# Source scores of eight end groups looked up two batches early, their rows gathered last, and end batches of 12, 13, 9 and 12 groups

## The chip, the core and the metric

The kernel runs on one core of one Trainium2 chip. The metric is device time in microseconds (us). The engines are named as in the profile: PE is the matrix engine (PEld its weight loads), DVE the vector engine, ACT the scalar engine, POOL the engine that issues the indirect gathers, SP the engine that issues most plain transfers.

## The reference

One graph attention layer over 12,500 nodes and 400,000 edges with 64 features, the edges sorted by destination, and a residual with a layer norm behind it:

```python
h_src = nfeats[src]
h_dst = nfeats[dst]
z_att = jnp.concatenate([h_src, h_dst, efeats], axis=-1)
e = jax.nn.leaky_relu(z_att @ W_attn + b_attn, negative_slope=0.01)[:, 0]
m = jnp.concatenate([h_src, efeats], axis=-1) @ W_ne
emax = jax.ops.segment_max(e, dst, num_segments=N)
ex = jnp.exp(e - emax[dst])
denom = jax.ops.segment_sum(ex, dst, num_segments=N)
alpha = ex / denom[dst]
z = jax.ops.segment_sum(alpha[:, None] * m, dst, num_segments=N)
out = jax.nn.relu(jnp.concatenate([nfeats, z], axis=-1) @ W_out)
return out
...
x = _layernorm(x + _L0_gnn_ref(x, edge_attr_64, ...), axis=-1)
```

## The kernel before, in words

**Groups, lots, batches.** The edges are cut into 782 groups of 512 (128 partitions by 4; the last has 32 partitions). The first 128 groups ("dense") have few destinations and are done without gathering a row per edge. The other 654 groups are worked in 42 batches of up to 16 groups; a batch is four lots of up to four groups. `ENDS` gives the lots of the last batches: (3,3,3,3), (3,3,3,3), (2,2,1,1), and all earlier ones are (4,4,4,4). Batches are numbered from 0, so the last four are 38 (16 groups), 39 (12), 40 (12) and 41 (6). "39.2" below is the lot with index 2 of batch 39.

**One batch.** (a) Gathers: for each group four indirect DMAs on POOL (`gather`, L331) each fetch 128 rows of `table`, which hold a node's source score, its features and two ones, into a `zx` tile. There are eight `zx` tiles, one per lot, so a gather of batch k starts when the same lot of batch k-2 has been multiplied. Up to batch 38 some gathers also wait by hand for marked PE steps of the batch before (`BEHIND`). (b) Scores, lot by lot (`scores`, L371 to L392): ACT copies the destination scores' window and the edge rows, DVE forms edge score + source score (column 0 of `zx`, L381) + destination score. (c) The softmax over the batch, written as a generator that yields four times: it starts with a transpose on DVE (L695) and ends with the transpose at L757. Between them PE turns columns to rows and back (L599, L602), and at each yield `dense_step` puts in other work: up to three pieces of the products of the batch before. (d) Weights (L792) for all lots, then the products on PE: of the first two lots at once, of the other two inside the next batch's softmax (`later`). A group takes four matmuls, in the trace eight passes (L809; in the last two batches L813, in two halves of 64 rows, eight matmuls and sixteen passes), and a lot one small L804 for its ones. (e) `add_in` (L818 to L828) moves the sums of a lot from PSUM to the ring `acc` of node sums, and blocks of nodes that are complete go through `finish0` to `finish3` (PE L1010, L1043, L1053; ACT L1018; DVE L1072 and on).

**The source score by a look.** For the dense groups a source score is not gathered. With src = 128 h + l, ACT makes an indicator over l from a row of the l's (`low_of`, which SP loads broadcast to all partitions; L431, L432), PE multiplies it with the 128 by 98 table of scores (`look_products`, L442: four matmuls, eight passes), and DVE picks the column h and adds it (`look_scores`, L469 to L475). The dense groups' looks end long before the last batches.

**Order.** The order on PE, DVE, ACT, SP and POOL is the order in which the program is written. Each engine takes its instructions in that order, so an instruction that waits holds all behind it.

Of the kernel before, what the change touches and what calls it, by code (L numbers as in the profile page):

```python
# [10 lines left out]
I32 = mybir.dt.int32  # L11
# [5 lines left out]
T = 4  # L17
# [33 lines left out]
NOW = 2  # L51
HALF = 2
# [7 lines left out]
def sorted_path(ctx, tc, x, dst, idx, edge, w_ne, w_attn, b_attn, w_out, out, flag):  # L60
# [29 lines left out]
    ENDS = ((3, 3, 3, 3), (3, 3, 3, 3), (2, 2, 1, 1))  # L90
# [16 lines left out]
    NK = len(sizes)  # L107
    SOON = (starts[1] - 1) // P + 1
# [13 lines left out]
    def kept_at(g):  # L122
        d = round_of(g)
        return g - begins[d] + d % 2 * BD
# [36 lines left out]
    low_rows = dram.tile([DG, P, T], BF16, name="low_rows")  # L161
# [182 lines left out]
    def ahead_of(g0, n, b0):  # L344

        Sk = widths[starts.index(b0)]
        if g0 not in early and b0 == starts[-1]:
            m = follows[g0][1]
            joint_ = edges(g0, n + m)
            early[g0], early[g0 + n] = joint_[:, 0:n], joint_[:, n:n + m]  # L350
# [9 lines left out]
    def rows_of(g0, n):  # L360

        assert g0 + n < NG or n == 1
        return RP if g0 + n == NG else P

    def scores(g0, n, zx, drel, b0, plain):
# [15 lines left out]
        nc.vector.tensor_tensor(ysum[0:r, 0:n], ysum[0:r, 0:n], zx[0:r, 0:n, :, 0], op=OP.add)  # L381
# [83 lines left out]
    def look_scores(g, found):  # L465
# [4 lines left out]
                                high[:, :, g:g + 1].to_broadcast([P, T, NB]), op=OP.is_equal)  # L470
# [330 lines left out]
    def products(k, pg, zx, w, groups, r=P, n=None):  # L801

        if n:
            nc.tensor.matmul(pg[0:1, 0:n, 0:2 * T], ident[0:1, 0:1], zx[0:1, 0:n, :, EW - 1:EW + 1],  # L804
                             start=True, stop=True)
# [60 lines left out]
    nc.sync.dma_start(out=ids, in_=idx[0:DG])  # L866
    nc.sync.dma_start(out=meet, in_=dst[DG * GE - 1:DG * GE + 1].unsqueeze(0))
# [9 lines left out]
    with before:  # L877
# [23 lines left out]
        with tc.manual_schedule(engines={EngineType.DVE, EngineType.Pool, EngineType.Activation, EngineType.PE, EngineType.SP}):  # L901
# [63 lines left out]
            nc.sync.dma_start(out=low_rows, in_=low_row)  # L965
            of_dense = dense_list()
            dense_places(of_dense, fit)
            nc.vector.tensor_copy(of_next[:, 2:4], meet)
# [144 lines left out]
    with loop:  # L1113
# [3 lines left out]
        for k, parts in enumerate(ENDS, len(sizes) - len(ENDS)):  # L1117
            lots[k] = [(starts[k] + sum(parts[:i]), n) for i, n in enumerate(parts)]
        flat = [(g0, n, b0) for b0, lot in zip(starts, lots) for g0, n in lot]
# [15 lines left out]
        def some_products():  # L1135

            if later:
# [3 lines left out]
                products(k, pg, zx, w, range(g, upto), n=n if g == 0 else None)  # L1141
# [27 lines left out]
        with tc.manual_schedule(engines={EngineType.PE, EngineType.DVE, EngineType.Activation, EngineType.SP, EngineType.Pool}):  # L1169
# [14 lines left out]
            for k, G in enumerate(sizes):  # L1184
# [7 lines left out]
                if k:  # L1192
                    joined = resting
                    batch_looks = alike(looks, ())
                    batch_counts = alike(counting)
                    if batch_looks and batch_looks[-1] + 1 in begins:
# [11 lines left out]
                tiles = [ahead.pop(0) if ahead else gather(g0, n, srcs, b0, k == 0, behind_of) for g0, n in lots[k][:3]]  # L1208
                parts = []
                after = node_z = None  # L1210
                for i, (g0, n) in enumerate(lots[k]):
                    if i == 3:
# [639 lines left out]
```

## Time and the profile before

| | |
|---|---|
| median of 3 runs | 4620.77 us (4603.75 to 4627.97) |
| the profiled execution | 4592.69 us |
| its span | 4591.0 us |
| mean granted PE clock | 0.653 of full |
| end of batch 40's softmax to start of batch 41's | 17.82 us |
| start of the last softmax to the end of the span | 41.6 us |

A row of a timeline gives the start in us from the span's start, the duration, the engine, the line and operation, out<-in with shapes, how many instructions were joined in the row, and in brackets the idle time of the engine before it with what ended it. A row of the windows gives a stretch, its length, the busy time of each engine with its instruction count, then the PE clock, the DMA engines' busy share and GB/s.

### The profile page before, as it was taken

To read this page: it belongs to the slowest core of one execution; us is meant where nothing else is said; L and a number is where in the kernel's file an instruction comes from. 1 tells how busy PE (TensorE), PEld (TensorE's weight loads), DVE (VectorE), ACT (ScalarE), POOL (GpSimd) and SP (SyncE) were. 2 spreads that over 40 slices of the span, in tenths; PEclk is the share of its full clock that TensorE was granted. 3 is DMA by queue.
4 is the path that set the end of the run, shared out by engine and by line. 5 is a ranking of instruction groups with operands and counts; after the bars stand their busy time and mean duration, and the time that the engine had idled before them with its cause. 6 is when DMAs were issued, how large, how long until landed. Compare 5 with 4: busy or idle time off the path is not lost. (4 is left out here: it accounts for less than half of the span.)

```text
span 4591.0 us, 39135 instructions
## 1 busy us (share of the span) xinstructions
PE 2467.7 (54%) x10315; PEld 2017.7 (44%) x10315; DVE 2171.1 (47%) x5618; ACT 1364.4 (30%) x2963; POOL 2480.1 (54%) x2644
## 2 busy tenths in 40 slices
PE   0135455565566666666556555455455555555554
PEld 0135445454454445454444444334344444444454
DVE  4444444454445545455444454443444444444355
ACT  0111123243323323343333332232333333333212
POOL 7566655565554554645464646555454545565542
PEclk9999985555556556666666655556566656666655
DMA  8222322232222222222132222222221212222211
GB/s 111 64 56 60 76 61 60 58 78 58 58 62 62 62 55 50 64 48 64 39 69 44 60 59 54 52 54 45 45 59 43 61 37 54 49 51 50 43 37 35
DMA packets 452952, 257.79 MB, mean 56 GB/s; under 512 B 266314, under 2 KB 410801, under 8 KB 452722
## 3 DMA queue, kind: packets, MB, share of 16 engines
q1 hardware_dynamic: 367036, 167.23, 14.6%
q0 software_dynamic: 83936, 87.27, 11.6%
q8 instruction: 87, 1.43, 0.1%
q14 instruction: 143, 1.17, 0.1%
q10 hardware_dynamic: 1750, 0.70, 0.1%
HBM read 248.17 MB, written 6.80 MB: 56 GB/s over the span
## 5 line engine op out<-in xcount | busy, mean ns | idle before, releaser
L331 POOL DMA_INDIRECT zx<-table,srcs x2552 | 2409.8, 944 | 2026.9 <-issue 813.8
L809 PE MATMUL pg<-w,zx 128*128 128x16 f32 (+9 forms) x5088 | 1055.4, 376 | 174.0 <-issue 124.2
L809 PEld LDWEIGHTS pg<-w,zx 128*128 128x128 f32 x5088 | 1040.8, 312 | 189.4 <-issue 127.7
L491 PE MATMUL pg<-big,lows 128*128 128x490 f32 (+3 forms) x1024 | 608.6, 751 | 731.8 <-DVE lows L486 266.1
L491 PEld LDWEIGHTS pg<-big,lows 128*128 128x128 f32 x1024 | 278.9, 292 | 996.4 <-issue 598.0
L483 ACT ACTIVATE big<-places,place 128x490 f32<-128x490 int16 (+3 forms) x512 | 317.9, 621 | 597.4 <-remote 323.9
L376 DVE TENSOR_REDUCE fixed<-pr 128x16 f32<-128x1024 f32 (+2 forms) x168 | 201.5, 1199 | 302.9 <-ACT fixed L371 206.4
L442 PE MATMUL pg<-s_src,big 128*128 128x98 f32 x1024 | 280.4, 440 | 81.1 <-issue 80.5
L599 PE MATMUL lines<-ident,bnd 128*1 128x128 f32 x168 | 48.2, 387 | 499.7 <-ACT bnd L702 291.8
L471 DVE TENSOR_TENSOR pr<-pr,pg 128x392 f32<-128x392 f32 x128 | 72.0, 562 | 511.2 <-PE pg L442 312.4
L442 PEld LDWEIGHTS pg<-s_src,big 128*128 128x128 f32 x1024 | 255.3, 328 | 81.7 <-issue 81.3
L484 ACT ACTIVATE big<-big 128x490 f32<-128x490 f32 (+3 forms) x512 | 277.3, 542 | 16.3
L828 DVE TENSOR_TENSOR acc<-acc,pg 128x16 f32 (+9 forms) x654 | 121.7, 186 | 315.7 <-remote 205.9
L568 PE MATMUL pg<-xall,counts 128*128 128x256 f32 (+1 forms) x650 | 193.6, 447 | 121.1 <-issue 120.8
L599 PEld LDWEIGHTS lines<-ident,bnd 128*1 128x1 f32 x168 | 12.4, 96 | 521.0 <-ACT bnd L702 307.7
L371 ACT ACTIVATE fixed<-wrow 128x144 f32<-128x144 f32 (+8 forms) x168 | 44.3, 263 | 660.2 <-issue 188.9
L486 DVE TENSOR_SCALAR lows<-fixed,low,kept 128x128 f32<-128x128 f32 x512 | 175.7, 404 | 125.1 <-remote 103.3
L568 PEld LDWEIGHTS pg<-xall,counts 128*128 128x128 f32 (+1 forms) x650 | 146.2, 228 | 159.8 <-issue 137.5
L374 DVE TENSOR_TENSOR pr<-ze,lines 128x1024 f32<-128x1024 f32 (+2 forms) x168 | 198.7, 1183 | 5.0 <-DMA ze<-in_edge_dram 4.9
L552 PE MATMUL pg<-wd,ep 128*128 128x10 f32 (+5 forms) x512 | 107.9, 325 | 141.8 <-issue 141.7
L372 ACT ACTIVATE zx<-ze 128x1024 f32<-128x1024 f32 (+2 forms) x168 | 174.0, 1036 | 5.9 <-DMA zx<-table,srcs 1.0
L552 PEld LDWEIGHTS pg<-wd,ep 128*128 128x128 f32 x512 | 111.8, 306 | 143.5 <-issue 143.5
(308 smaller groups left out, 2715.3 us busy)
## 6 DMA issues: line engine op xcount, KB each, us to landing
ze<-in_edge_dram SPq DMA_DIRECT2D x157, 512.0 KB
zx<-table,srcs POOLq DMA_INDIRECT x2552
low_of<-low_rows SPq DMA_DIRECT2D x128, 128.0 KB
ep<-in_edge_dram SPq DMA_DIRECT2D x128, 128.0 KB
wrow<-wins SPq DMA_DIRECT2D x152, 96.0 KB
ed<-in_edge_dram SPq DMA_DIRECT2D x14, 640.0 KB
ed<-in_edge_dram SPq DMA_DIRECT2D x14, 384.0 KB
table<-xall SPq DMA_DIRECT2D x7, 455.0 KB
```

What stands on the lines that cost most here:

```text
L331: row = nc.gpsimd.indirect_dma_start(out=zx[0:r, g, t, 1:EW] if plain else zx[0:r, g, t, 0:EW], out_offset=None, in_=x[:, :] if plain else ...
L372: nc.scalar.activation(zx[0:r, 0:n, :, EW:EW + D], ze[0:r, 0:n], AF.Copy)
L374: nc.vector.tensor_tensor(pr[0:r, 0:n], ze[0:r, 0:n], w_edge[0:r].unsqueeze(1).to_broadcast([r, n, T, D]), op=OP.mult)
L376: nc.vector.tensor_reduce(ysum[0:r, 0:n], pr[0:r, 0:n], axis=AX.X, op=OP.add)
L442: nc.tensor.matmul(found[:, t, :], hot[:, :, t], s_src, start=True, stop=True)
L483: nc.scalar.activation(hi, places[:, 0:wide], AF.Square, bias=place[:, t, g:g + 1])
L484: nc.scalar.activation(hi, hi, AF.Relu, scale=-1.0, bias=1.0)
L486: nc.vector.tensor_scalar(lows[t], count_, low[:, t, g:g + 1], kept[:, t, kept_at(g):kept_at(g) + 1], op0=OP.is_equal, op1=OP.mult)
L491: nc.tensor.matmul(to, lows[t], highs[t], start=(t == 0), stop=(t == T - 1))
L552: nc.tensor.matmul(z[:, h:h + 2], rows_, cols, start=(i == 0), stop=(i + 1 == len(steps)), skip_group_check=True).ins
L568: nc.tensor.matmul(pairs[0:m * ND, 0:m * D], counts[:, h0:h0 + m, :].rearrange("l h n -> l (h n)"), xall[:, h0:h0 + m, 1:EW], start=(h0 == ...
L809: nc.tensor.matmul(pg[:, g, :], zx[:, g, t, 1:EW + D], w[:, g, t, :], start=(t == 0), stop=(t == T - 1)).ins
```

## The change

`ENDS` becomes (3,3,3,3), (4,3,3,3), (3,2,2,2), (3,4,4,1). The number of batches and the groups in the last four are the same; batch 38 has 12 groups (16 before), 39 has 13 (12), 40 has 9 (12), 41 has 12 (6). As `ENDS` has four entries now, batch 38 no longer takes the `BEHIND` waits.

For lots 1 and 2 of the last batch (eight groups) the source scores come from looks: four in batch 39, four in batch 40, the first in the batch's scoring and three in the yields of its softmax. The add in `scores` (L381) of these lots then reads `y_dense` instead of column 0 of `zx`; ACT's copy of the edge rows into the other columns of the same `zx` tile (L372) stays. The last batch's gathers are issued in the order lot 0, lot 3, lot 1, lot 2, and its lots are scored in the order 1, 2, 0, 3. The rows are still gathered, since the products need them; these come last, in the order of landing, one group at a time for the looked-up lots. At the start of the kernel a load, one DVE and one ACT operation and a store prepare the eight rows of `low_rows`.

```diff
-    ENDS = ((3, 3, 3, 3), (3, 3, 3, 3), (2, 2, 1, 1))
+    ENDS = ((3, 3, 3, 3), (4, 3, 3, 3), (3, 2, 2, 2), (3, 4, 4, 1))
+DIRECT = (1, 2)
...
+    L0 = starts[-1] + sum(ENDS[-1][:DIRECT[0]])
+    NL = sum(ENDS[-1][i] for i in DIRECT)
...
+    def direct(g0):
+        return L0 <= g0 < L0 + NL
...
     def ahead_of(g0, n, b0):
-        if g0 not in early and b0 == starts[-1]:
-            m = follows[g0][1]
-            joint_ = edges(g0, n + m)
-            early[g0], early[g0 + n] = joint_[:, 0:n], joint_[:, n:n + m]
...
-        nc.vector.tensor_tensor(ysum[0:r, 0:n], ysum[0:r, 0:n], zx[0:r, 0:n, :, 0], op=OP.add)
+        of_src = y_dense[:, :, g0 - L0:g0 - L0 + n].rearrange("p t g -> p g t") if direct(g0) else zx[0:r, 0:n, :, 0]
+        nc.vector.tensor_tensor(ysum[0:r, 0:n], ysum[0:r, 0:n], of_src, op=OP.add)
...
+        by_landing = [lot for lot in lots[-1] if not direct(lot[0])] + [lot for lot in lots[-1] if direct(lot[0])]
+        lots[-1] = [lot for lot in lots[-1] if direct(lot[0])] + [lot for lot in lots[-1] if not direct(lot[0])]
...
+                    if NK - 3 <= k < NK - 1:
+                        first_ = DG + (k - NK + 3) * NL // 2
+                        batch_looks = list(range(first_, first_ + NL // 2))
...
+                if final:
+                    landing = {g0: gather(g0, n, srcs, b0, False) for g0, n in by_landing}
+                    tiles = [landing[g0] for g0, _ in lots[k]]
...
+                    if k == NK - 3 and i == 1:
+                        of_end = lists[NK - 1][:, L0 - starts[-1]:L0 - starts[-1] + NL]
+                        nc.vector.tensor_scalar(of_end[:, :, T:2 * T], of_end[:, :, 0:T], 7, None, op0=OP.logical_shift_right)
+                        nc.scalar.activation(high[:, :, 0:NL], of_end[:, :, T:2 * T].rearrange("p g t -> p t g"), AF.Copy)
+                        nc.vector.memset(y_dense[:, :, 0:NL], 0.0)
...
                     if k and i == 1 and (batch_looks or batch_counts or joined is not None):
                         add_up()
...
+                        if direct(g0):
+                            for g in range(n):
+                                products(k, pg, zx, w, [g], n=(g, g + 1))
+                        else:
+                            products(k, pg, zx, w, range(n), rows_of(g0, n), (0, n))
```

The condition of the `add_up()` shown as context is true in batches 39 and 40 now: the sums of the first two lots of the batch before are added to `acc` after the second lot's scores, and no longer in the softmax.

On PE, in the softmax of batch 40 before, from its first transposition of columns to rows (`L599`) to the last of rows to a column (`L602`), the products of batch 39's lots 2 and 3 lie between them:

```order
L599 MATMUL lines<-ident,bnd 1x4x32 x2
L804 MATMUL pg<-zx,ident 1x3x8
L809 MATMUL pg<-w,zx 128x48 x12
L602 MATMUL lines<-ident,line 128x1 x2
L804 MATMUL pg<-zx,ident 1x3x8
L809 MATMUL pg<-w,zx 128x48 x8
L599 MATMUL lines<-ident,bnd 1x4x32 x2
L809 MATMUL pg<-w,zx 128x48 x4
L602 MATMUL lines<-ident,line 128x1 x2
```

The same place after the change (the lines are numbered six or seven higher: `L605` is the old `L599`, `L816` the old `L809`, `L448` the old `L442`):

```order
L605 MATMUL lines<-ident,bnd 1x4x32 x2
L811 MATMUL pg<-zx,ident 1x3x8
L816 MATMUL pg<-w,zx 128x44 x12
L448 MATMUL pg<-s_src,big 128x98 x4
L608 MATMUL lines<-ident,line 128x1 x2
L811 MATMUL pg<-zx,ident 1x3x8
L816 MATMUL pg<-w,zx 128x44 x8
L448 MATMUL pg<-s_src,big 128x98 x4
L605 MATMUL lines<-ident,bnd 1x4x32 x2
L816 MATMUL pg<-w,zx 128x44 x4
L448 MATMUL pg<-s_src,big 128x98 x4
L608 MATMUL lines<-ident,line 128x1 x2
```

The pieces of products stay where they were; behind each stands a look of four matmuls, ahead of the next transposition.

On ACT, the scores of the last batch before, between them the work of two blocks of nodes (`L1018` copies a transposed block that PE made at L1010, `L660` and `L661` read penalties from PSUM, `L1078` belongs to a layer norm). In the brackets stand the semaphores waited for: `DMASW` of the gathers, `DMAHW` of plain transfers:

```order
L371 ACTIVATE fixed<-wrow 128x96 [waits DMAHW1_49,DVE_49]
L372 ACTIVATE zx<-ze 128x8x64 [waits DMASW5_49,DMASW4_49,DMASW6_49,DMASW3_49,DMASW7_49,DMASW2_49,DMAHW0_49,DMASW1_49,DMASW0_49]
L1078 ACTIVATE pr<-yo 128x256 [waits DVE_49]
L660 ACTIVATE rw<-pps 1x256 [waits PE_49]
L661 ACTIVATE rw<-pps 1x256
L1018 ACTIVATE xtt<-pg 64x256 [waits PE_49]
L1018 ACTIVATE xtt<-pg 64x256
L371 ACTIVATE fixed<-wrow 128x96 [waits DMAHW2_49,Activation_49]
L372 ACTIVATE zx<-ze 128x8x64 [waits DMASW4_49,DMASW5_49,DMASW3_49,DMASW6_49,DMASW2_49,DMASW7_49,DMASW1_49,DMASW0_49]
L1018 ACTIVATE xtt<-pg 64x128 [waits PE_49]
L1018 ACTIVATE xtt<-pg 64x128
L371 ACTIVATE fixed<-wrow 128x48 [waits DMAHW5_49,DVE_49,Activation_49]
```

And after it (`L1032` is the old `L1018`, `L376` and `L377` the old `L371` and `L372`):

```order
L376 ACTIVATE fixed<-wrow 128x192 [waits DMAHW1_49,DVE_49]
L377 ACTIVATE zx<-ze 128x16x64 [waits DMASW5_49,DMASW4_49,DMASW6_49,DMASW3_49,DMASW7_49,DMASW2_49,DMAHW0_49,DMASW1_49,DMASW0_49]
L1092 ACTIVATE pr<-yo 128x256 [waits DVE_49]
L666 ACTIVATE rw<-pps 1x256 [waits PE_49]
L667 ACTIVATE rw<-pps 1x256
L1032 ACTIVATE xtt<-pg 64x256 [waits PE_49]
L1032 ACTIVATE xtt<-pg 64x256
L376 ACTIVATE fixed<-wrow 128x192 [waits DMAHW4_49,Activation_49]
L377 ACTIVATE zx<-ze 128x16x64 [waits DMASW5_49,DMASW4_49,DMASW6_49,DMASW3_49,DMASW7_49,DMASW2_49,DMAHW3_49,DMASW1_49,DMASW0_49]
L1032 ACTIVATE xtt<-pg 64x128 [waits PE_49]
L1032 ACTIVATE xtt<-pg 64x128
L376 ACTIVATE fixed<-wrow 128x144 [waits DMAHW6_49,DVE_49,Activation_49]
```

The two block copies keep their places: the first stands ahead of the second lot's scores, which are now those of a looked-up lot of four groups. ACT's copies of edge rows into `zx` (`L377`) wait for all eight semaphores of the gathers in the looked-up lots as they did before; only the add on DVE has another operand.

36 lines of the change are left out of this document (24 added, 12 removed).

## The prediction

> **What bounds the kernel now.** I read the page's totals first, then windows over the last four batches, then the timelines of POOL, ACT and DVE there.
>
> ```profile
> span 4591.0 us, 39135 instructions
> PE 2467.7 (54%) x10315; PEld 2017.7 (44%) x10315; DVE 2171.1 (47%) x5618; ACT 1364.4 (30%) x2963; POOL 2480.1 (54%) x2644
> L331 POOL DMA_INDIRECT zx<-table,srcs x2552 | 2409.8, 944 | 2026.9 <-issue 813.8
> ```
>
> No engine is full: POOL, PE and DVE are busy about half of the time and hand work round a circle (gather, scores, softmax, products, free buffer). So the change is worth what it does to that circle in the last batches. Two kinds of DVE rows divide them: the transpose L695 starts a softmax, called S below, and L757 ends it, called F. S38 and S39 stand first, then F39, S40, F40, S41 and F41.
>
> ```profile
> 4376.03 0.32 DVE L695 STREAM_TRANSPOSE turned<-soft 128x128 f32<-128x128 f32 x1
> 4450.20 0.24 DVE L695 STREAM_TRANSPOSE turned<-soft 128x128 f32<-128x128 f32 x1
> 4471.78 0.33 DVE L757 STREAM_TRANSPOSE fixed<-turned 128x128 f32<-128x128 f32 x1
> 4514.46 0.24 DVE L695 STREAM_TRANSPOSE turned<-soft 128x128 f32<-128x128 f32 x1
> 4531.61 0.33 DVE L757 STREAM_TRANSPOSE fixed<-turned 128x128 f32<-128x128 f32 x1
> 4549.43 0.24 DVE L695 STREAM_TRANSPOSE turned<-soft 128x128 f32<-128x128 f32 x1
> 4564.84 0.33 DVE L757 STREAM_TRANSPOSE fixed<-turned 128x128 f32<-128x128 f32 x1
> ```
>
> This gives S38 to S39 74.2 us, S39 to F39 21.6, F39 to S40 42.7, S40 to F40 17.15, F40 to S41 17.8, S41 to F41 15.4, and 26.2 from F41 to the end of the span.
>
> The surprise is in the windows: start and end, length, then busy time and count of PE, PEld, DVE, ACT, POOL.
>
> ```profile
> core 0: us, PE busy (x) PEld busy (x) DVE busy (x) ACT busy (x) POOL busy (x), PEclk, DMA share, GB/s
> 4321.70:4336.50 14.80, 14.60 (x60) 12.85 (x60) 11.71 (x19) 8.38 (x19) 11.30 (x12) 0.76 0.58 148
> 4336.50:4362.00 25.50, 4.98 (x12) 2.84 (x11) 0.27 (x2) 1.47 (x3) 18.86 (x20) 0.55 0.17 27
> 4386.90:4406.60 19.70, 15.29 (x74) 14.26 (x73) 14.34 (x40) 3.48 (x10) 15.13 (x16) 0.50 0.18 28
> 4406.60:4420.00 13.40, 1.21 (x6) 1.73 (x6) 1.57 (x4) 0.00 (x0) 7.57 (x9) 0.50 0.36 93
> 4461.70:4481.00 19.30, 15.26 (x74) 14.36 (x74) 13.80 (x41) 3.49 (x10) 14.72 (x16) 0.50 0.21 39
> 4481.00:4495.00 14.00, 1.44 (x7) 1.49 (x6) 0.95 (x1) 0.00 (x0) 7.91 (x9) 0.50 0.36 74
> 4496.50:4516.50 20.00, 4.47 (x21) 4.31 (x21) 16.49 (x34) 8.41 (x19) 15.41 (x16) 0.50 0.43 94
> ```
>
> Each pair of rows is one long run of gathers. PE does 60, 74 and 74 passes in its first part and then 12, 6 and 7 in the next 25.5, 13.4 and 14.0 us, with DVE and ACT idle beside it. The last row, a run of 16 gathers in which PE had only 21 passes to do, shows no such stall. When it ends is told by ACT, which waits for PE's block (first two rows), and by POOL: the ends of the runs ahead of these, the start of the next, and the last batch's own.
>
> ```profile
> 4420.83 0.76 ACT L1018 ACTIVATE xtt<-pg 64x256 f32<-64x256 f32 x2 [17.41 <-remote]
> 4495.54 0.76 ACT L1018 ACTIVATE xtt<-pg 64x256 f32<-64x256 f32 x2 [18.74 <-PE pg L809]
> 4360.36 0.94 POOL L331 DMA_INDIRECT zx<-table,srcs  x1 [0.30 <-issue]
> 4415.66 0.94 POOL L331 DMA_INDIRECT zx<-table,srcs  x1 [0.30 <-issue]
> 4490.41 0.94 POOL L331 DMA_INDIRECT zx<-table,srcs  x1 [0.30 <-issue]
> 4523.50 0.94 POOL L331 DMA_INDIRECT zx<-table,srcs  x1 [6.99 <-issue]
> 4533.09 0.87 POOL L331 DMA_INDIRECT zx<-table,srcs  x1 [0.30 <-issue]
> ```
>
> ACT goes on 5.17 us behind the last gather of 39.3 (4415.66) and 5.13 behind that of 40.3 (4490.41). I read it so: in a run of gathers, one per 1.25 us (0.94 + 0.30), PE gets some 60 to 75 passes through and is then held until about 5.1 us after the run's last gather. Why, the trace does not tell. By the Trainium skill ("SBUF — State Buffer", section "Who interferes with whom") DMA never contends with a compute engine and "PE and ACT never wait on anyone". The rows disagree: 6 passes in 13.4 us, and ACT idle for 17.41 us.
>
> The wait that the change is about, the last batch's scores behind its gathers, does not decide in this profile: the last gather starts at 4533.09, and S41 comes 16.3 us later, at 4549.43. Nor is it all removed. The add on DVE has another operand, but ACT's copy of edge rows goes into the tile that the gathers fill, and the page's group shows it released by them:
>
> ```profile
> L372 ACT ACTIVATE zx<-ze 128x1024 f32<-128x1024 f32 (+2 forms) x168 | 174.0, 1036 | 5.9 <-DMA zx<-table,srcs 1.0
> ```
>
> The order shows that wait kept for the looked-up lots. DVE scores the first of them without it, but on ACT all later lots' windows are queued behind the copies of both.
>
> **The change part by part.** The price of a look, from one of the dense groups (ACT, then PE, then DVE):
>
> ```profile
> 3724.86 0.70 ACT L431 ACTIVATE big<-low_of,p_col 128x512 f32<-128x512 bf16 x1
> 3725.60 0.63 ACT L432 ACTIVATE big<-big 128x512 f32<-128x512 f32 x1
> 3729.59 2.14 PE L442 MATMUL pg<-s_src,big 128*128 128x98 f32 x8
> 3731.77 0.56 DVE L471 TENSOR_TENSOR pr<-pr,pg 128x392 f32<-128x392 f32 x1 [7.11 <-PE pg L442]
> 3732.37 0.56 DVE L473 TENSOR_REDUCE picked<-pr 128x4 f32<-128x392 f32 x1
> 3732.97 0.17 DVE L475 TENSOR_TENSOR y_dense<-y_dense,picked 128x4 f32<-128x4 f32 x1
> 3735.27 0.55 DVE L469 TENSOR_TENSOR pr<-fixed,high 128x392 f32<-128x392 f32 x1
> ```
>
> That is 1.33 us of ACT, 2.14 of PE and 1.84 of DVE (0.55 + 0.56 + 0.56 + 0.17), eight times. No scoring falls away for it: the score still does every operation, with another operand in one add. And the price of a lot's scores and products:
>
> ```profile
> 4266.74 1.22 DVE L374 TENSOR_TENSOR pr<-ze,lines 128x1024 f32<-128x1024 f32 x1
> 4272.31 0.18 DVE L392 TENSOR_TENSOR soft<-fixed,sdst 128x16 f32<-128x16 f32 x1
> 4540.73 0.69 DVE L374 TENSOR_TENSOR pr<-ze,lines 128x512 f32<-128x512 f32 x1
> 4544.29 0.17 DVE L392 TENSOR_TENSOR soft<-fixed,sdst 128x8 f32<-128x8 f32 x1
> 4325.15 11.15 PE L568 MATMUL pg<-xall,counts 128*128 128x256 f32 x42
> 4517.40 5.35 PE L809 MATMUL pg<-w,zx 128*128 128x48 f32 x24
> 4566.37 1.95 PE L813 MATMUL pg<-w,zx 128*64 128x48 f32 x32
> ```
>
> A lot of four is scored in 5.75 us, of two in 3.73, so about 1.0 per group; three take 4.7 and the 32-row group about 2.4 by that line. Products of batch 39's kind take 5.35/24 = 0.22 us per pass, 1.8 per group; the last batch's 0.98 per group.
>
> Front of the kernel: one 32 KB load, one DVE and one ACT operation, a store of 8 rows, some 1 us in all on queues with idle time around them. I take 0; if nothing covers it, +1. SP also gets eight more broadcast loads and loses a joined edge load; they are issued a look ahead, and if one comes late it is the look that is late, which T3's upper end holds. Then, in us against before:
>
> T1, start of batch 38's softmax. Its runs of gathers shrink: batch 39 still gets its first lots here, now 4+3 groups (28 gathers, not 24), but batch 38 has no fourth groups. The run that ended at 4360.36 begins later (its buffers belong to batch 37's first lots) and ends at the same time, so the node products (L568, 42 passes and the smaller ones) are held as before. One group less in the last lot: -1.3, plus some of the shorter run: -4. Ends: -20, if those products all pass before the stall (most of the 25.5 us row), and +4, if the run ends later.
>
> T2, S38 to S39. The last two lots of batch 39 are 24 gathers as before, so the hold stays. One group more to score (+1.0), one look's DVE work (+1.84) between scores: +3. Ends: -2 (the added `add_up` leaves the softmax and lies idle here) to +7 (also PE's 2.14 and 1.8 us).
>
> T3, softmax of batch 39. Three looks of 2.14 us on PE ahead of its transposes are 6.4, with 1.2 for the DVE parts that aren't beside PE; the products that stand there lose a piece (batch 38's lots 2, 3 have six groups, not eight; one half-lot of those lies beside other work): -1.8. Sum +6, ends +3 to +9.
>
> T4, F39 to S40. Batch 40 has 9 groups, its last two lots 16 gathers for 24. The run that started at 4461.70 (S39+11.5) then ends near S39+31, which is F39+4, so most of the 14.0-us stall goes: -9.5. Three groups fewer to score: -3. A look's 1.84 and about 1 for the adds pulled ahead: +3. Sum -10; ends -12 and -2 (the stall only moves into the next run, 16 gathers).
>
> T5, S40 to S41, the term that decides. Softmax 40 gets three looks: 6.4 + 1.2 = 7.6, so it takes 24.8. The last batch's lots 1 and 2 use the buffers of 39.2 and 39.3. In the trace 41.2's first gather starts 9.04 us behind S40 (4523.50 - 4514.46); there are 8 gathers in that run before, 32 after. The last is issued at S40 + 9.0 + 31 x 1.247 = S40 + 47.7, and PE is held until S40 + 52.8. Its passes in that time exceed the 60 to 75: by my count of the order, 52 up to the softmax's last transposes, 71 with the node block's, then 80 for batch 40's first five groups. Behind them stands the block that ACT's L1018 copies, and behind that ACT's part of the second looked-up lot. From the release on come that lot (5.75), the lot of three (4.7) and the 32-row lot (2.4): S41 at S40 + 65.6, where it was 35.0. That is +31. Ends: if PE is not held, ACT's copy for lot 2 still waits for the last gather, S40 + 47.7 + 0.9 and then lands, by my estimate at S40 + 50; behind it the copy (1.0), the block's two copies (0.76), lot 0's window (0.3), the later half of its scores (1.9, by the rows above) and the 32-row lot (2.4): S41 at S40 + 56.5, T5 = +22. If that copy held nothing either, F40 to S41 would be the 5.6 us that it has now beside its scores (17.8 - 2 x 3.7 - 2 x 2.4) and 18.6 of scores: S40 + 49, +14. Upward +36, if the release comes 5 us later.
>
> T6, softmax 41: batch 40's late lots have 2+2 groups for 3+3, partly beside waits: -1. Ends -3 to +2.
>
> T7, F41 to the end: 12 groups' products for six. Six groups x 0.98 = 5.9, and a small matmul per looked-up group, 6 more at 0.1 to 0.2: +7; ends +4 to +9 (the adds follow PE). The gathers are no wait here: the last lands near S40 + 50, F41 is at S40 + 81.
>
> Sum: -4 + 3 + 6 - 10 + 31 - 1 + 7 = +32. Against the profiled execution's 4592.69 (its span is 4591.0) that is 4625. It lay 28 us under the median of the runs, 4620.77, which the comparison uses, so I add the 32 there: 4652.8. What a measurement of this kernel can tell from no change is about 0.5%, 23 us.
>
> **The rivals.**
>
> First, on the other side: not slower, since no run of gathers holds PE in these batches any more. It is decided by how many gathers a run must have. For it: the run of 16 at 4496.50 went by without a stall, and batch 40's become 16. Against it: 39.2 with 39.3 is still a run of 24, and the last is 32; both runs of 24 above stalled alike. Then T1 is -20, T2 -10 (3 less the 13.4 us stretch), T3 +6, T4 -10, T5 +22, T6 -1, T7 +7: -6, 4615.
>
> Second: only the last batch's PE is not held; it is decided by whether PE's 60th to 75th pass behind S40 + 9 comes before S40 + 47.7. Then ACT's copy sets T5, +22, and the sum is +23: 4644, on the bound between slower and no change. For it: many of those passes wait for DVE and ACT anyhow, and the slow phase needs a busy PE so far as the rows show. Against it: 151 passes are due. This would also be the time if the rule of the Trainium skill named above held and the stalls of batches 38 and 39 had another cause than gathers.
>
> Third: batch 38's node products slip through, T1 = -20 in place of -4: +16, 4637. For it: 60 passes went by in 4321.70 to 4336.50, and 12 were left; against it: that run's end does not move.
>
> Fourth: the looks' passes come in the held stretches, where PE passes one instruction per 1 to 2 us (25.5 us for 12, 14.0 for 7), so that both softmaxes wait and T3 and T5 take their upper ends, with T2 at its own: +3 +5 +4 = 12 more, +44, 4665.
>
> Fifth: the change does in full what it says: ACT's copy gates nothing, no run holds PE, and the looks lie where PE waits for the softmax's other engines. T1 -20, T2 -10, T3 0, T4 -10, T5 +6 (14 less the 7.6), T6 -1, T7 +7: -28, 4593. For it: PE is only 54% busy. Against it: the order, and the runs of 24.
>
> **How the numbers follow.** Forecast (+32) 0.38; fourth (+44) 0.11; second (+23) 0.18; third (+16) 0.12; first (-6) 0.13; fifth (-28) 0.08. Slower by over 0.5%: 0.38 + 0.11 + half of the second, 0.58. Within 0.5%: the other half, third and first, 0.34. Faster: 0.08. The range leaves out the fifth and a part of the first below (its T7 or T3 at their low ends), and above what goes beyond the fourth with 8 us for the front and T1's upper end: 4606 to 4673.
>
> **What would show it.** In the changed kernel's profile: S40 to S41 near 66 us with a PE stretch of a few passes in 14 us or more and an ACT wait of over 10 us ahead of L1018's successor; release about 5 us behind the last gather; F39 to S40 near 33 without a stalled stretch; softmaxes of 39 and 40 near 27.5 and 25; 33 from F41 to the end. Wrong would be: S40 to S41 near 57 with PE at work throughout and ACT's copy released by the last gather (second rival), no stretch of few passes anywhere (first), or S38 earlier by 15 or more (third). If the stall depends on something else than passes within a run, say on how much other traffic runs, T4 and T5 both fall.

## The result, and the profile after

The changed kernel takes 4652.98 us (median of 20 runs, 4617.81 to 4687.78), the kernel before 4620.39 (20 runs, 4582.47 to 4659.99): ratio 1.0074 (of the fast runs), 95% interval 1.005 to 1.0098. By the medians it is 0.71% slower, where 0.69% was forecast; single runs scatter by some 40 us either way, so that the median agrees with the forecast to a fraction of a microsecond is luck. The profiled execution took 4641.19 us, 48.5 more than the one whose rows the forecast's terms were read from, so that in the profiles the terms add up to 16.5 us more than the +32 of the forecast. Chips differ in a way that every number below needs: on chips 3, 11 and 2 of the study the kernel before takes 3340 to 3347 us; on chip 5 it takes 4597, near the 4620 of the chip of the first measurement ("the first chip" below).

The page's totals first, of after:

```profile
span 4639.5 us, 39406 instructions
PE 2485.5 (54%) x10415; PEld 2027.5 (44%) x10415; DVE 2186.9 (47%) x5655; ACT 1374.7 (30%) x2981; POOL 2478.2 (53%) x2644
L337 POOL DMA_INDIRECT zx<-table,srcs x2552 | 2408.4, 944 | 2066.4 <-issue 874.6
```

100 PE passes, 37 DVE and 18 ACT instructions are new; PE is busy 18 us longer, DVE 16, and the span is 48.5 us longer. The starts and ends of the softmaxes (L701 is the old L695, L763 the old L757), S38, S39, F39, S40, F40, S41, F41:

```profile
4379.90 0.24 DVE L701 STREAM_TRANSPOSE turned<-soft 128x128 f32<-128x128 f32 x1
4459.86 0.24 DVE L701 STREAM_TRANSPOSE turned<-soft 128x128 f32<-128x128 f32 x1
4486.17 0.33 DVE L763 STREAM_TRANSPOSE fixed<-turned 128x128 f32<-128x128 f32 x1
4522.04 0.24 DVE L701 STREAM_TRANSPOSE turned<-soft 128x128 f32<-128x128 f32 x1
4567.27 0.33 DVE L763 STREAM_TRANSPOSE fixed<-turned 128x128 f32<-128x128 f32 x1
4591.79 0.24 DVE L701 STREAM_TRANSPOSE turned<-soft 128x128 f32<-128x128 f32 x1
4607.81 0.33 DVE L763 STREAM_TRANSPOSE fixed<-turned 128x128 f32<-128x128 f32 x1
```

| stretch | before | after | differs by | forecast |
|---|---|---|---|---|
| to S38 | 4376.0 | 4379.9 | +3.9 | -4 |
| S38 to S39 | 74.2 | 80.0 | +5.8 | +3 |
| softmax 39 | 21.6 | 26.3 | +4.7 | +6 |
| F39 to S40 | 42.7 | 35.9 | -6.8 | -10 |
| S40 to S41 | 35.0 | 69.8 | +34.8 | +31 |
| softmax 41 | 15.4 | 16.0 | +0.6 | -1 |
| F41 to the end | 26.2 | 31.7 | +5.5 | +7 |

The term that decides is S40 to S41, and within it softmax 40: 45.2 us for 17.15. Windows of after there (the columns are those of the prediction's windows):

```profile
4531.00:4543.00 12.00, 11.53 (x54) 10.80 (x53) 6.29 (x19) 2.76 (x7) 9.18 (x10) 0.50 0.17 32
4543.00:4568.00 25.00, 0.00 (x0) 0.00 (x0) 4.65 (x15) 0.10 (x1) 18.34 (x21) 0.50 0.16 25
4568.00:4576.20 8.20, 5.41 (x36) 4.72 (x36) 7.55 (x11) 1.57 (x3) 2.69 (x3) 0.50 0.31 74
```

PE does 54 passes in 12 us and none in the next 25, while POOL goes on gathering. The rows at the edges, of POOL's run, of PE, of ACT and of DVE:

```profile
4531.08 0.95 POOL L337 DMA_INDIRECT zx<-table,srcs  x1 [15.48 <-issue]
4570.36 0.94 POOL L337 DMA_INDIRECT zx<-table,srcs  x1 [0.30 <-issue]
4540.02 2.15 PE L448 MATMUL pg<-s_src,big 128*128 128x98 f32 x8
4542.55 0.37 PE L608 MATMUL lines<-ident,line 1*128 1x1 f32 x2 [0.39 <-ACT line L612]
4567.90 0.29 ACT L774 ACTIVATE keep<-part,dens 1x1 f32<-1x1 f32 x1 [25.40 <-DVE turned L761]
4568.24 0.26 PE L608 MATMUL lines<-ident,keep 1*128 1x1 f32 x1 [25.32 <-issue]
4576.19 1.11 PE L820 MATMUL pg<-w,zx 128*64 128x48 f32 x17 [1.15 <-issue]
4559.40 0.56 DVE L477 TENSOR_TENSOR pr<-pr,pg 128x392 f32<-128x392 f32 x1 [17.19 <-remote]
4565.07 0.36 DVE L756 SCALAR_TENSOR_TENSOR soft<-mask,lines,soft 128x128 f32<-128x128 f32 x1 [2.84 <-remote]
```

The run starts 9.04 us behind S40, as foreseen. By PE's rows the third look ends at 4542.17 and the transposes behind it at 4542.92, yet DVE, which reads their results, goes on only at 4559.40 and 4565.07. The trace also keeps times at which PE's semaphore rose, though not all: 4559.38 and 4564.98 are among them, just ahead of these two starts, with none between 4539.64 and the first. So PE's results are late, and not DVE. Here the hold does not stand in PE's rows, as it did before (one pass per some 2 us), but in the wait of the engine that reads what PE has made. PE's 25.32 us without a row end 0.05 us behind ACT's `L774`, whose result the next transpose reads: they are DVE's wait handed on. Both late results come ahead of the run's last gather, and from F40 to S41 DVE waits for 1.0 us in all. PE is at full pace for good at 4576.19, 5.8 us behind the last gather, but S41 does not wait for that.

### The profile page after: what moved, and what is told of

Same layout as the page of the kernel before. It is cut to its first block, busy times and chain, and to the rows that moved or that the text cites. A ratio compares the mean times of both kernels' runs of the same rounds, so it can differ in the third digit from the quotient of the medians.

```text
span 4639.5 us, 39406 instructions
## 1 busy us (share of the span) xinstructions
PE 2485.5 (54%) x10415; PEld 2027.5 (44%) x10415; DVE 2186.9 (47%) x5655; ACT 1374.7 (30%) x2981; POOL 2478.2 (53%) x2644
## 5 line engine op out<-in xcount | busy, mean ns | idle before, releaser
L816 PE MATMUL pg<-w,zx 128*128 128x44 f32 (+8 forms) x5064 | 1052.4, 377 | 162.7 <-issue 117.4
L816 PEld LDWEIGHTS pg<-w,zx 128*128 128x128 f32 x5064 | 1036.9, 313 | 181.0 <-issue 120.1
L448 PE MATMUL pg<-s_src,big 128*128 128x98 f32 x1088 | 297.7, 440 | 119.6 <-issue 119.4
L381 DVE TENSOR_REDUCE fixed<-pr 128x16 f32<-128x1024 f32 (+2 forms) x168 | 201.5, 1199 | 284.7 <-ACT fixed L376 194.3
L448 PEld LDWEIGHTS pg<-s_src,big 128*128 128x128 f32 x1088 | 272.5, 328 | 118.7 <-issue 118.5
L605 PE MATMUL lines<-ident,bnd 128*1 128x128 f32 x168 | 47.8, 384 | 494.5 <-ACT bnd L708 316.0
L490 ACT ACTIVATE big<-big 128x490 f32<-128x490 f32 (+3 forms) x512 | 277.3, 542 | 16.3
L376 ACT ACTIVATE fixed<-wrow 128x96 f32<-128x96 f32 (+10 forms) x168 | 44.2, 263 | 678.3 <-DVE pr L475 197.3
L605 PEld LDWEIGHTS lines<-ident,bnd 128*1 128x1 f32 x168 | 12.4, 96 | 516.6 <-ACT bnd L708 333.0
L515 DVE TENSOR_TENSOR counts<-counts,pg 128x490 f32 (+3 forms) x128 | 74.9, 585 | 234.5 <-remote 127.0
L377 ACT ACTIVATE zx<-ze 128x1024 f32<-128x1024 f32 (+2 forms) x168 | 174.0, 1036 | 5.7 <-issue 1.0
L502 ACT ACTIVATE big<-places,place 128x98 f32<-128x98 int16 x240 | 69.8, 362 | 292.0 <-remote 142.9
```

The lines of the kernel that those rows point to most:

```text
L377: nc.scalar.activation(zx[0:r, 0:n, :, EW:EW + D], ze[0:r, 0:n], AF.Copy)
L381: nc.vector.tensor_reduce(ysum[0:r, 0:n], pr[0:r, 0:n], axis=AX.X, op=OP.add)
L448: nc.tensor.matmul(found[:, t, :], hot[:, :, t], s_src, start=True, stop=True)
L490: nc.scalar.activation(hi, hi, AF.Relu, scale=-1.0, bias=1.0)
L816: nc.tensor.matmul(pg[:, g, :], zx[:, g, t, 1:EW + D], w[:, g, t, :], start=(t == 0), stop=(t == T - 1)).ins
```

## The experiments

**The dispute by itself, and the first chips.** The theory says that a run of gathers holds PE: few passes get through, or their results come late, until some 5 us behind the run ("the hold" from here on). That was measured alone, in a kernel that leaves out the layer (the comments in the code shown in this section are added).

```diff
+        passes(800)        # nc.tensor.matmul(pg, a, w, start=True, stop=True)
+        gathers(0, 240)    # indirect_dma_start, 128 rows of 64 each
```

> A kernel for the disputed wait alone, which leaves out the layer: 800 matmuls of 128 by 48 (1600 passes) on PE beside 240 gathers of 128 rows on POOL, with no dependence between the two but a common start. Theory (the hold is real and also there without the profiler): PE does 60 to 75 passes, then about one instruction per gather (1.25 us) for 299 us, then the other 1400 passes at 0.14 to 0.22 us: 500 to 620 us. Rival (the stalls of the profile belong to the recording, or to waits of this kernel that the trace does not name): both run at once, 300 to 370 us, and PE's rows run through at 0.14 to 0.22 us per pass.

361.8 us on chip 3: the rival. The windows of PE's and POOL's work:

```profile
20.00:60.00 40.00, 40.00 (x189) 40.00 (x190) 0.00 (x0) 0.00 (x0) 30.21 (x33) 1.00 0.14 27
60.00:200.00 140.00, 140.00 (x658) 140.00 (x658) 0.00 (x0) 0.00 (x0) 105.87 (x113) 1.00 0.14 27
```

4.7 passes per us all along, beside a gather each 1.25 us. But this chip isn't like the first one: before takes 3340.39 us on it.

> The same 800 matmuls and 240 gathers, the gathers behind the last matmul, so that nothing overlaps: by both theories the sum, 225 to 350 us of matmuls and 299 of gathers, 525 to 670 us. By the theory the kernel with both at once is less than 70 us faster than this one, by the rival 220 or more.

474.1 us, and not the reference that it was to be: only the last 88 gathers ended up behind the matmuls, the other 152 beside them (POOL stands still for 152.5 us between). What it gives is PE's pace without gathers, from a window in which POOL stands still:

```profile
210.00:350.00 140.00, 140.00 (x658) 140.00 (x658) 0.00 (x0) 0.00 (x0) 0.00 (x0) 1.00 0.00 1
```

658 passes in 140 us, as many as beside the gathers.

> The 800 matmuls beside 240 gathers again, in case this is a chip where the kernel before takes 4600 us. Theory there: 60 to 75 passes, then one instruction per gather or two until 5 us behind the last gather, then the rest: 500 to 620 us for the 361.8 that it took where before takes 3340. Rival (the gathers alone don't hold PE, something else of the kernel does): 360 to 370 us on that chip too. Where before takes 3340: 361.8 again.

361.82 us, on chip 2, where before takes 3347.13. So the matmuls and gathers by themselves were never on a chip with the hold; whether gathers alone cause it there stays open.

**The change and its parts where before takes 3340 us.** First the sizes alone:

```diff
-        return L0 <= g0 < L0 + NL
+        return False                       # direct(): no lot is looked up
...
-                    if NK - 3 <= k < NK - 1:
+                    if False:              # no looks
...
-                    if k == NK - 3 and i == 1:
+                    if False:              # nothing prepared for looks
```

> The end batches of 12, 13, 9 and 12 groups alone: no looks, every score reads its gathered rows, the last batch in the order of its lots. Theory (a run of gathers lets PE do 60 to 75 passes, then holds it until some 5 us after the run): the last batch's lots 0 and 1 (28 gathers) and lots 2 and 3 (20) make one run that ends about 37 us behind the start of batch 40's softmax, PE is held until 42, scores of lots 2 and 3 follow the gathers; start of softmax 40 to start of softmax 41 in 55 to 65 us; with the shorter batch 40 the sum is +10 to +30 us against before, so 0 to 20 less than the whole change. Rival (the looks' 16 passes-and-picks in the two softmaxes are what costs): within 5 us of before or below it, 30 us less than the whole change.

3337.52 us, ratio 0.9992 (0.9982 to 1.0001): no difference, as the rival has it (within 5 us of before). S40 to S41 takes 56.5 us, inside the theory's 55 to 65, but not for its reason: beside the gathers PE does 111 passes in 13 us (3251 to 3264). What this trace has is a wait that the first profile lacked: with 12 groups in the last batch its scores do wait for their gathers. DVE's rows between F40 and S41:

```profile
3264.06 0.18 DVE L387 TENSOR_TENSOR fixed<-fixed,zx 128x16 f32<-128x16 f32 x1 [1.11 <-DMA zx<-table,srcs]
3284.00 0.18 DVE L387 TENSOR_TENSOR fixed<-fixed,zx 128x16 f32<-128x16 f32 x1 [14.12 <-DMA zx<-table,srcs]
3288.50 0.16 DVE L387 TENSOR_TENSOR fixed<-fixed,zx 32x4 f32<-32x4 f32 x1 [0.30 <-DMA zx<-table,srcs]
```

15.5 us in all. The looked-up lots are there to remove this wait.

```diff
-                    if NK - 3 <= k < NK - 1:
+                    if False:              # no looks; the scores read zeros
```

> The change without its eight looks; the scores of the two lots read zeros in their place, so the order, the late gathers and the sizes stay. Theory (PE held by the run of 32 gathers): softmax 40 has 24 passes fewer behind the start of the run, some 35, and so slips through in about 18 us, but batch 40's first products (80 passes) are then caught, and softmax 41 starts 60 to 66 us behind softmax 40, where the whole change has 69.8; in all 10 to 17 us less than the whole change, +15 to +25 against before. Rival (the looks' own work fills the 45 us of softmax 40): 17 us for softmax 40 and 42 to softmax 41, 35 to 40 us less than the whole change, faster than before.

3324.76 us, 0.9955 (0.9938 to 0.9971). F40 to S41 takes 23.9 us here and 39.3 with the sizes alone, 15.4 less: the wait is gone. By its words the rival's numbers came nearer (17.1 us for softmax 40, 41.0 to softmax 41), but on a chip without the hold, and the whole change lies 24 us above this run (next), not 35 to 40.

> The changed kernel itself once more, since the first four runs were on a chip where the kernel before takes 3340 us and where neither PE's rows beside gathers nor the softmaxes of the end batches stall. Theory (the stall belongs to the chip or its state, and the change's price on the first chip was that stall in softmax 40): where the kernel before takes 3340, no stretch of a few passes, softmax 40 in 24 to 26 us, 14 to 20 us above the run without looks (3324.8), so 3339 to 3345, within 0.2% of before; where it takes 4620, again +0.5 to +1% with 40 us or more in softmax 40. Rival (the cost is the looks and sizes themselves, wherever it runs): +30 us or more at 3340 too.

3348.34 us on chip 11, 1.0024 (1.0014 to 1.0034): 7.9 us slower than before and 24 above the run without looks; the expectation was 3339 to 3345. Its S40, F40 and S41, and the window of its run of 32 gathers:

```profile
3250.81 0.24 DVE L701 STREAM_TRANSPOSE turned<-soft 128x128 f32<-128x128 f32 x1
3276.00 0.33 DVE L763 STREAM_TRANSPOSE fixed<-turned 128x128 f32<-128x128 f32 x1
3299.91 0.24 DVE L701 STREAM_TRANSPOSE turned<-soft 128x128 f32<-128x128 f32 x1
...
3259.80:3271.80 12.00, 11.48 (x54) 10.77 (x53) 6.99 (x21) 2.76 (x7) 9.21 (x10) 0.50 0.18 32
3271.80:3298.60 26.80, 11.43 (x111) 9.70 (x111) 24.14 (x46) 6.88 (x17) 20.10 (x23) 0.50 0.25 47
```

The first 12 us are those of the first chip pass for pass (54 passes, clock 0.50, 10 gathers); then PE goes on with 111 passes instead of none, and S40 to S41 takes 49.1 us, the value that the prediction gave for nothing held. The looks' price stands between this run and the one without: softmax 39 25.8 for 17.6, F39 to S40 33.5 for 26.1, softmax 40 25.2 for 17.1, together 23.7 us for the eight looks and the adds that they pull ahead.

**The run of gathers cut.** (The lines left out make a lot's first gather wait for the step of PE that `first` names.)

```diff
...
+                    firsts = {L0: steps_before[3], L0 + lots[k][0][1]: steps_before["second"]}
-                    landing = {g0: gather(g0, n, srcs, b0, False) for g0, n in by_landing}
+                    landing = {g0: gather(g0, n, srcs, b0, False, first=firsts.get(g0)) for g0, n in by_landing}
```

> The change with its long run of gathers cut: the first gather of the looked-up lot 1 waits for PE's last step in softmax 40, that of lot 2 for the products of batch 40's second lot. Theory: where runs of gathers hold PE (before at 4620), softmax 40 falls from 45 to 24 to 27 us, and S41 comes 50 to 60 us behind S40 in place of 69.8 (ACT's copies of edge rows now wait for the late gathers): 10 to 20 us less than the whole change. Where they don't (before at 3340), nothing is won in softmax 40, and the gathers, 16 us later, hold ACT's copies: 10 to 25 us more than the whole change. Rival (gathers don't matter to PE on any chip): the second result on both.

3348.7 us on chip 11, 1.0025 (1.0015 to 1.0035), as the whole change. That nothing is won without the hold was expected; that nothing is lost was not, and it disproves the step on ACT's copies. In the whole change's trace on this chip the copy of lot 2's edge rows runs while that lot's gathers are still being issued (ACT's row, and POOL's first and last of the lot):

```profile
3287.69 1.06 ACT L377 ACTIVATE zx<-ze 128x1024 f32<-128x1024 f32 x1
3279.83 0.94 POOL L337 DMA_INDIRECT zx<-table,srcs  x1 [0.30 <-issue]
3298.57 0.94 POOL L337 DMA_INDIRECT zx<-table,srcs  x1 [0.30 <-issue]
```

The copy does not wait for its own lot's gathers. What cutting does where PE is held was not measured.

**On a chip with the hold.** The next four runs were on chip 5.

> The kernel before, for its profile on a chip where it takes 3340 us, to read the change there interval by interval. Theory (no hold of PE there, so the queue of gathers is the bound): the start of softmax 38 to 39 and 39 to 40 take about 48 gathers x 1.247 = 60 us each, none with a stretch of few passes; the change then has 68 and 59 there, and 49 for 35 from softmax 40 to 41. Rival (the last batches are bound by DVE and PE there too): they take 64 to 74 us, as on the first chip, and the gathers stand still between.

4585.47 us there, so that the expectation, which was for a chip of 3340, was not put to the test. The trace has the first one's intervals again: S38 to S39 74.1 us, S39 to S40 64.0, S40 to S41 35.0 (first chip 74.2, 64.3 and 35.0), and the stalls (74 passes in each run's first part, then 7 in 13.4 and 8 in 14.0 us). As the changed kernel has the hold on the first chip and not on chip 11, it takes something of the chip, or of what surrounds it, and not the program alone.

What surrounds it may be the recording, a rival that no run tests. Every run on record has a recorded span and clock beside its time, and the recordings of the two kinds of chip differ: this kernel's traces from the first chip and chip 5 keep 2.3 to 2.5 semaphore updates (the events that end waits) per gather, those from chips 2, 3 and 11 15.9. With the updates missing, the profile puts long waits down to "remote", a releaser that it cannot name, in the first kind alone. One group of ACT's, from the page of the changed kernel on the first chip and from that on chip 11:

```profile
L489 ACT ACTIVATE big<-places,place 128x490 f32<-128x490 int16 (+3 forms) x512 | 317.9, 621 | 568.2 <-remote 366.2
L489 ACT ACTIVATE big<-places,place 128x490 f32<-128x490 int16 (+3 forms) x512 | 317.2, 619 | 107.8 <-PE pg L497 66.9
```

Whether PE is held, and the kernel takes 4600 us, when nothing is recorded stays open.

```diff
-                    if NK - 3 <= k < NK - 1:
-                        first_ = DG + (k - NK + 3) * NL // 2
-                        batch_looks = list(range(first_, first_ + NL // 2))
+                    if NK - 8 <= k < NK - 4:
+                        first_ = DG + (k - NK + 8) * NL // 4
+                        batch_looks = list(range(first_, first_ + NL // 4))
...
```

> The change with its eight looks earlier: two in each of batches 34 to 37 (full batches of 64 gathers, 79.9 us each where the kernel takes 3340), none in 39 and 40; all else as in the change, and nothing left out. Theory (a look costs only where its batch isn't bound by gathers: 8.3 and 8.1 us in softmaxes 39 and 40, 7.4 between them): the full batches stay at 80 us, and the time is that of the run without looks, 3323 to 3330, 15 us faster than before. Rival (a look costs its DVE and PE time wherever it stands, 2 to 4 us each): 3338 to 3350. On a chip where before takes 4620: 20 us or more less than the change.

4653.1 us, 1.0145 (1.01 to 1.019): slower than before by more than the change itself, against the expectation. The full batches are not bound by gathers on such a chip (94 to 119 us each from S33 to S37, in both profiles of before, for 64 gathers of 1.25), and with two looks each they grow: S33 to S37 takes 479.1 us, and 433.7 and 432.0 in the next two runs, which have the looks in the change's places, on the same chip. But the end tells most about the forecast. Softmax 40, now without looks, takes 17.1 us, and S41 still comes 66.5 us behind S40. PE's rows behind F40, with the run's last gather and the copy of ACT that waits for PE's block:

```profile
4564.90 1.41 PE L820 MATMUL pg<-w,zx 128*64 128x48 f32 x21
4568.15 0.24 PE L820 MATMUL pg<-w,zx 128*64 128x48 f32 x1 [1.85 <-issue]
4570.25 0.24 PE L820 MATMUL pg<-w,zx 128*64 128x48 f32 x1 [1.86 <-issue]
...
4596.85 0.34 PE L820 MATMUL pg<-w,zx 128*64 128x48 f32 x1 [0.36 <-issue]
4597.55 0.89 PE L820 MATMUL pg<-w,zx 128*64 128x48 f32 x12 [0.36 <-issue]
...
4591.35 0.94 POOL L337 DMA_INDIRECT zx<-table,srcs  x1 [0.30 <-issue]
4602.07 0.55 ACT L1032 ACTIVATE xtt<-pg 64x128 f32<-64x128 f32 x2 [16.43 <-PE pg L1024]
```

and the windows that hold them:

```profile
4552.60:4566.40 13.80, 10.29 (x65) 9.16 (x65) 11.32 (x30) 3.20 (x8) 10.42 (x12) 0.50 0.22 51
4566.40:4596.90 30.50, 3.56 (x15) 2.59 (x16) 10.08 (x15) 2.98 (x7) 19.79 (x21) 0.50 0.18 30
```

65 passes, then 15 in 30.5 us, then full pace at 4597.55, 6.2 us behind the last gather; ACT waits for 16.43 us, and lot 0's later scores and the 32-row lot follow. This is the forecast's picture but for one step: the second looked-up lot is scored while PE is held, and in its place behind the release stand 4.5 us of passes that PE has left. It shows that the looks are not what makes S40 to S41 long: without them the hold moves behind the softmax, and only 3.9 us are saved of the 70.4 that a run with the looks takes on this chip (the last of these four).

```diff
...
+                        for _ in range(10 if (k, n) == (NK - 2, 2) else 0):
+                            look_products(hot_, bank_)
...
```

> The change with PE kept busy in softmax 40 by ten more repeats of the third look's matmuls (80 passes, 21.4 us at 0.267 each), in place of the stall of 17.2 + 5 us that the first profile has there. Theory (that stall alone makes the 69.8 us between softmaxes 40 and 41 of 49): the interval grows to 69 to 72 us, and the time to 3367 to 3372, 0.8 to 0.95% over before, as on the first chip. Rival (a stall there is taken up later, since gathers or products are waited for anyhow): under 10 us more than the change.

4662.15 us (median of 2), 1.0153. It was meant for a chip without the hold, to put a stall in by hand, and landed on one with it, so it settles nothing between its two expectations. S40 to S41 takes 92.4 us. The windows:

```profile
4540.00:4560.00 20.00, 20.00 (x93) 19.10 (x93) 7.15 (x22) 4.66 (x10) 10.22 (x11) 0.50 0.26 56
4560.00:4590.00 30.00, 8.13 (x29) 7.85 (x29) 0.00 (x0) 0.00 (x0) 19.99 (x22) 0.50 0.15 24
4590.00:4612.00 22.00, 15.28 (x97) 14.56 (x97) 9.54 (x22) 1.68 (x3) 0.00 (x0) 0.53 0.03 8
```

Once more a slow stretch of 30 us, this time in PE's rows and inside softmax 40; PE is at full pace at 4591.72, 6.3 us behind the last gather (4585.45), and does there what it hadn't done by then. F40 to S41 takes 23.9 us behind it.

```diff
-                    if k and i == 1 and (batch_looks or batch_counts or joined is not None):
+                    if k and i == 1 and (batch_looks and batch_looks[0] < DG or batch_counts or joined is not None):
```

> The change without the adds of finished sums pulled ahead in batches 39 and 40; they stay in the softmax as before the change. Theory (DVE's 3.0 us of adds stand in the way in batch 40's scoring, and its later rows wait for them): 2 to 5 us less than the change. Rival (the softmax has to do them then, where the looks already fill DVE's gaps): within 1 us of the change.

4616.5 us, 1.0043 (1.0014 to 1.0072), where the whole change has 1.0074 (1.005 to 1.0098) on the first chip: the intervals overlap, so the few microseconds are not resolved. In the trace F39 to S40 takes 30.8 us, with the adds pulled ahead 35.9 on the first chip and 35.5 in the run before this one, on the same chip. S40 to S41 takes 70.4, of which softmax 40 has 38.8, and PE is at full pace 4.5 us behind the last gather.

**A version faster than before, on one kind of chip.** The edits of the early looks and of the cut together.

> The eight looks two per batch in batches 34 to 37, and the run of 32 gathers cut as in the run with the cut alone: lot 1's first gather behind PE's last step in softmax 40, lot 2's behind the products of batch 40's second lot. Theory on a chip where before takes 3340 us (no hold): the looks cost nothing in full batches, which gathers bound at 80 us, and the cut nothing in the end: 3323 to 3332, 0.3 to 0.5% faster than before. On a chip where it takes 4600 (hold): with early looks alone softmax 40 took 17.1 us and the next 49.3 went by under the hold; cut, no run is longer than 16 gathers, PE isn't held, softmax 40 to 41 takes 41 to 48 us for 66.4, and the end comes about 25 to 35 us behind the last gather; against before +0.4 to +1.2%, since the looks slow the full batches there. Rival (what holds PE isn't the length of the run): 60 us or more from softmax 40 to 41 there.

3334.82 us on chip 2, 0.9964 (0.995 to 0.9977): 12 us faster than before. The looks aren't free in full batches even here (those from 33 to 37 take 82 us in the mean, 79 in the change on chip 11), but softmaxes 39 and 40 are back at 17.6 and 17.1 us. On a chip with the hold the early looks without the cut lost 1.45%; the two together were not measured there.

## Why the prediction was right

**The hold (T5) came as forecast in cause and in sum, but not by the path, and the sum owes a part to luck.** PE was to be free for some 60 to 75 passes, 52 of them up to the softmax's last transposes, so that softmax 40 would pass and S41 would wait for a release 5.1 us behind the last gather. On the first chip 54 passes were free, and the hold caught the softmax's own last results: 45.2 us in place of 24.8, 20.4 more. F40 to S41 then took 24.5, which is the 24.2 given for the case that nothing is held, and 16.3 less than the 40.8 of the forecast. What S41 hangs on are results that came 11.0 and 5.4 us ahead of the start of the last gather, and no release behind it. Two errors that nearly cancel gave 69.8 for 65.6. The signs named ahead say the same: a stretch without passes is there, but ACT's wait stands ahead of `L774` (25.40 us) and not ahead of `L1032`, the old `L1018`.

With the looks taken out of that softmax 65 passes were free, and the hold fell where the forecast had it, with ACT's wait and 66.5 us for 65.6. In the four profiles with a run of 32 gathers and the hold, PE is at full pace 4.5 to 6.3 us behind the last gather (forecast 5.1). That the run of gathers is what holds PE is argued from their place in time; it was neither cut on a chip with the hold, nor measured there without the layer.

**The second rival's +22 was wrong**, and with it "ACT's copy for lot 2 still waits for the last gather": the copies run ahead of the gathers of their own lot. The semaphores in the order's brackets were read as those of this lot's gathers; the trace says that the copy did not wait for all of them. The page's group, read as a sign of that wait, has 1.0 us of it for 168 copies together. Where PE isn't held, S40 to S41 is 49.1 us, the value kept there as a further end (+14). The fifth rival's "ACT's copy gates nothing" holds; its other two conditions don't.

**The looks (T3, part of T4, T5).** 7.6 us for three looks in a softmax was forecast, 8.3 and 8.1 are the difference on chips without the hold. T4 was mis-sized: the stalled stretch went, as forecast, but the sum is -6.8 for -10. On chip 11 one look and the adds pulled ahead made F39 to S40 7.4 us longer, where 3 were put down; 3.0 of it are the adds and 3.9 a wait of DVE for ACT's copy of a window, which the prediction did not have.

**T1 and T2.** To S38 +3.9 for -4: but softmax 37 started 4.9 us later already, and the kernel before started it 5.1 us earlier in another execution (4267.4, chip 5), so from S37 on it is -1.0. S38 to S39 +5.8 for +3, inside its bounds. T6 and T7 came out within 2 us.

**"The wait that the change is about, the last batch's scores behind its gathers, does not decide in this profile"** held and is the deeper reason: the wait for gathers is not in before; the sizes bring it (15.5 us on chip 3), the looks take it away again (15.4) and cost 23.7. On chips 3 and 11 +8 us is left of the change (1.0024), by the medians -2.9 for the sizes, -12.8 for the lots that don't wait and +23.6 for the looks with the adds that they pull ahead. On the first chip the hold comes on top: S40 to S41 is 20.7 us longer there than on chip 11. That the time moves by this alone is argued from the traces; the run that was to put the stall in by hand did not show it.

The section weighed in the prediction (the Trainium skill, "SBUF — State Buffer", section "Who interferes with whom": PE and ACT never wait on anyone) speaks of the ports of SBUF. The runs on chip 11 (111 passes beside the run of 32) and on chips 3 and 2 agree with it. The first chip and chip 5 (15 passes in 30.5 us) would speak against it only if the hold were a matter of those ports, which no run here shows; and ACT's 17.41 us, which the prediction held against it, were a wait for PE's block that the program asks for.

## What to carry to other kernels

Price a stretch by the wait that ends last in it, and ask of each moved transfer which run it joins: here the order that frees the scores from their gathers puts 32 gathers into one run, and where PE is held its results come late beside it. A lookup that replaces a gathered value must be cheaper than the wait that it removes, and that wait has to be in the profile of the kernel as it is, not in that of sizes chosen for the lookup. Measure on more than one chip, and if it can be done without a recording, before a stall is called a property of the program. And compare a forecast term by term: a sum can be right by errors that cancel.

## What was not expected of the hardware

- The same program takes 3340 to 3347 us on chips 3, 11 and 2 and 4597 on chip 5. A gather takes 944 to 947 ns on both kinds, and DVE is busy 2166 to 2187 us on both; in the rows read here PE's progress beside a run of gathers differs. The cause is open (the recording is one candidate): neither the granted clock (0.50 in the same window of both) nor the gathers' own duration differs.
- From S33 to S37 a batch takes 76 to 80 us in the changed kernel on chip 11, about 64 x 1.247, and 94 to 119 in the kernel before on the first chip and chip 5: what bounds the whole kernel changes with the chip.
- A hold can be missing from the rows of the engine that is held: PE's rows end at 4542.92, while its semaphore rises at 4559.38 and 4564.98, and DVE goes on at 4559.40 and 4565.07. In the run with early looks it is the same: PE's product that DVE's `L1086` reads ends at 4563.95 by its rows, the semaphore rises at 4575.14, and DVE starts at 4575.17.
